# A second level of the seven-product scheme in the last stage of a transformer layer, for three of its four units

## The chip, the cores and the metric

The kernel runs on one core of one Trainium2 chip. A core has TensorE (matrix multiply; in the profile PE for the matmuls and PEld for the loads of the stationary operand), VectorE (DVE), ScalarE (ACT), GpSimd (POOL) and SyncE (SP), which here only starts transfers. The engines run their own instruction queues in order and wait for each other through semaphores. TensorE writes to PSUM, of which a partition has eight banks of 2 KB, and the other engines read it from there.

The metric is the device time in microseconds (us). Before the change the median of three runs is 739.32 us (737.54 to 741.06).

## The reference

All data is float32. `x` has 2 batches of 1024 tokens of 512 features. What is computed is one layer:

```python
xn = layernorm(x)
# attention without softmax: q, k = elu(.) + 1 of xn @ wq.T + bq and xn @ wk.T + bk, v = xn @ wv.T + bv, 16 heads of 32
KV = einsum('bhsd,bhse->bhde', k, v)
attn = (einsum('bhsd,bhde->bhse', q, KV) / (q . sum_s(k) + 1e-8)) @ wo.T + bo
# feed-forward with low-rank terms, shared and for 8 experts of rank 8, two of which are chosen for a token
gate = xn @ W_gate + lora + expert_lora
up   = xn @ W_up   + lora + expert_lora
hidden = silu(gate) * up                     # 1376 features
ffn  = hidden @ W_down + lora + expert_lora
out  = x + attn + ffn
```

The change concerns the end of it: `hidden @ W_down`, the attention's last product (queries, already divided, times a matrix that holds both KV and wo), their low-rank terms, and the sum with `x`.

## The kernel before, in words

Earlier stages normalise and transpose `x`, project keys and queries, fold KV and wo into one matrix for each batch (`kvo_dram`), and compute the hidden features. Hidden and query features are left in DRAM in a layout made for the last stage (`h_dram`, `q_dram`, and `r_dram` for the 96 hidden features that don't fill a pair of chunks).

The last stage works through four units. Unit `u = 2 b + s` is batch `b`, half `s`: 512 tokens, as two blocks of 256. The contracted features come in seven pairs of 128-row chunks: five of hidden (`NP = 5`, weights `wd[0]` to `wd[4]`) and two of queries (`NPQ = 2`, weights `kvo[0]`, `kvo[1]`). The 512 output columns are two halves of 256. So for each pair of chunks there is a product of 2 x 2 blocks by 2 x 2 blocks, and it is done with seven block products in place of eight (the scheme of Strassen in Winograd's form). A feature tile `f` holds eight blocks of 256 columns: four that are loaded, and four sums of them, which VectorE makes (`feature_sums`, L1489 to L1492). A weight tile holds eight blocks in the same manner (`block_diffs`, L1370 to L1373, on GpSimd). `H_OF` and `B_OF` tell which block each product 1 to 7 takes.

`emit_unit` keeps all seven products of a unit open in seven PSUM banks at once (`po1` to `po7`), and the eighth bank, `held3`, holds `ph`, the low-rank input (L1620). The order on TensorE is written by hand: for each of the five hidden pairs all seven products, two matmuls each (one for each 128 tokens; the moving operand is 256 weight columns wide, L1597); then `ph`; then the two query pairs; then the low-rank terms `bd_sb` x `had` and the 96 left-over features `wdr` x `hr`. VectorE, ScalarE and GpSimd then combine the seven banks into four blocks of `x` that were loaded earlier (L1641 to L1647, L1666), and SyncE stores these (L1668). In the meantime the features of the next unit arrive in a ring of nine tiles (`RING`, L1484) and get their sums. In units before the last, the sums for the next unit lie in VectorE's queue partly ahead of the read-out and partly behind it.

A float32 matmul stands in the profile as two records, each with a weight load of its own: a unit's 98 block matmuls are 196 records.

The orders of PE, DVE, ACT and POOL are those of the program text; that of SP's transfers is planned by the framework.

Of the kernel before, what the change touches and what calls it, by code (L numbers as in the profile page):

```python
# [10 lines left out]
F32 = mybir.dt.float32  # L11
# [4 lines left out]
P = 128  # L16
# [21 lines left out]
def layer_kernel(  # L38
# [41 lines left out]
    TB = 512  # L80
# [20 lines left out]
    def pool(stack, name, bufs=1, **k):  # L101
        return stack.enter_context(tc.tile_pool(name=name, bufs=bufs, reuse_waits="tile", **k))
# [78 lines left out]

    n_sa = 2 * NC + FULL + 1
    n_sat = (n_sa + SG - 1) // SG
    sat = const.tile([P, n_sat, P], F32, name="sat")
    sa = p1.tile([P, n_sat * SG, 32], F32, name="sa")


# [304 lines left out]
    class Finish:  # L492


        def __init__(self, b, pg, ksum):
            self.b, self.pg, self.ksum = b, pg, ksum
            self.made = 0
# [666 lines left out]
    def held(name, k):  # L1164
        return ps_pool[0].tile([P, TB], F32, tag=f"held{k}", name=name)
# [251 lines left out]
    def load_kvo(b):  # L1417
        ws = []
        for j in range(NPQ):
            if j == 0:  # L1420
                t = tsp.tile([P, 8, 2 * P], F32, tag="t0", name=f"kvo{b}_0")
            else:
                t = tsp.tile([P, 8, 2 * P], F32, tag="t1", name=f"kvo{b}_1")
            for half in range(2):
                nc.sync.dma_start(
                    out=t[:, 2 * half : 2 * half + 2, :].rearrange("p s n -> p (s n)"),
                    in_=kvo_dram[b][:, j + half * NPQ, :],
                )
            ws.append(t)
        return ws  # L1430


    def load_last():
        sb = tsp.tile([P, D], F32, name="sb_d")
        for k in range(SG):
            nc.sync.dma_start(out=sb[k * 32 : k * 32 + RANK, :], in_=b_down[ER:LR, :])
        wdr = tsp.tile([REST + 1, D], F32, name="wdr")
        nc.sync.dma_start(out=wdr[0:REST, :], in_=w_down[RC, :])
        nc.sync.dma_start(out=wdr[REST : REST + 1, :], in_=b_down[LR : LR + 1, :])

        bd = tsp.tile([2 * ER, D], F32, name="bd_sb")
        for i in range(2):
            nc.sync.dma_start(out=bd[i * ER : (i + 1) * ER, :], in_=b_down[0:ER, :])
        diffs = [tsp.tile([w.shape[0], HD], F32, name=n) for w, n in ((wdr, "wdr_diff"), (bd, "bd_diff"))]
        return sb, wdr, bd, *diffs
# [34 lines left out]
    def load_feature(u, i):  # L1480
        at = RING[(NF * u + i) % len(RING)]
        t = (slots if at[0] == "s" else tsp).tile([P, 8, UT], F32, tag=at, name=f"f{u}_{i}")
        b, s = divmod(u, 2)
        nc.sync.dma_start(out=t[:, 0:4, :], in_=h_dram[b][i][s] if i < NP else q_dram[b][i - NP][s])  # L1484
        feats[u, i] = t

    def feature_sums(u, i):
        t = feats[u, i]
        nc.vector.tensor_add(t[:, 4, :], t[:, 1, :], t[:, 3, :])  # L1489
        nc.vector.tensor_sub(t[:, 6, :], t[:, 0, :], t[:, 1, :])  # L1490
        nc.vector.tensor_sub(t[:, 5, :], t[:, 4, :], t[:, 0, :])
        nc.vector.tensor_sub(t[:, 7, :], t[:, 2, :], t[:, 5, :])  # L1492
# [72 lines left out]
        feature_sums(0, i)  # L1565


    p4w = pool(ctx, "p4w", bufs=2)

    H_OF = {1: 0, 2: 2, 3: 7, 4: 3, 5: 4, 6: 5, 7: 6}  # L1570
    ORDER = (1, 6, 5, 2, 7, 3, 4)
    d1, d2 = slice(0, HD), slice(HD, D)

    def load_unit(u):

        b, s = divmod(u, 2)
        hr = p4w.tile([REST + 1, 2, UT], F32, tag="hr", name=f"hr{u}")
        nc.gpsimd.memset(hr[REST : REST + 1, :, :], 1.0)
        nc.sync.dma_start(out=hr[0:REST, 0:2, :], in_=r_dram[b][s])
        xr = []  # L1580
        for g in range(2):
            t = p4w.tile([P, NQ, D], F32, tag=f"xr{g}", name=f"xr{u}_{g}")
            first = b * BT + g * TB + s * UT
            nc.sync.dma_start(out=t, in_=x[first : first + UT, :].rearrange("(q p) d -> p q d", p=P))
            xr.append((t, first))
        return hr, xr

    def emit_unit(u, loaded, last):
        hr, xr = loaded
        b, s = divmod(u, 2)  # L1590
        ps = {
            p: (bank(f"po{p}_{u}") if i < 4 else held(f"po{p}_{u}", i - 4)).rearrange("p (q n) -> p q n", n=HD)
            for i, p in enumerate(ORDER)
        }

        def term(p, q, lhsT, rhs, start=False, stop=False):
            nc.tensor.matmul(ps[p][:, q, :], lhsT, rhs, start=start, stop=stop, skip_group_check=True)  # L1597

        def products(n, w):
            f = feats[u, n]  # L1600
            for p in ORDER:
                for q in range(NQ):

                    term(p, q, f[:, H_OF[p], ts(q, P)], w[:, B_OF[p], :],
                         start=(n == 0 and q == 0), stop=(n == NF - 1 and p in (1, 6, 5)))

        for n in range(NP):
            products(n, wd[n])
            if n == 1 and not last:
                for i in range(2):  # L1610
                    load_feature(u + 1, i)
                    feature_sums(u + 1, i)

        ph = held(f"ph{u}", 3)[:, 0:UT]
        chunks = [(feats[u, j][:, 2 * half : 2 * half + 2, :], ad_sb[:, j + half * NP, 0:ER])
                  for j in range(NP) for half in range(2)]
        chunks.append((hr[0:REST], ad_sb[0:REST, FULL, 0:ER]))
        for n, (f, a) in enumerate(chunks):
            for g in range(2):
                nc.tensor.matmul(  # L1620
                    ph[g * ER : (g + 1) * ER, :], a, f[:, g, :],
                    start=(n == 0), stop=(n == len(chunks) - 1), skip_group_check=True,
                )
        had = p4w.tile([P, UT], F32, tag="had", name=f"had{u}")
        for g in range(2):
            rows = slice(g * ER, (g + 1) * ER)
            nc.vector.tensor_mul(had[rows, :], ph[rows, :], wT[b][rows, g * TB + s * UT : g * TB + (s + 1) * UT])  # L1627
        if not last:
            for i in range(2, NF):
                load_feature(u + 1, i)  # L1630
        for i in range(NPQ):
            products(NP + i, kvo[i])
        if u == 1:
            kvo[:] = load_kvo(1)

        def tmp(name):
            return p4w.tile([P, NQ, HD], F32, tag=name, name=f"{name}_{u}")

        (x1, first1), (x2, first2) = xr
        a, u2, u4 = tmp("a"), tmp("u2"), tmp("u4")  # L1640
        nc.scalar.copy(a, ps[1])  # L1641
        nc.gpsimd.tensor_add(x1[:, :, d1], x1[:, :, d1], a)  # L1642
        nc.vector.tensor_add(u2, a, ps[6])
        nc.gpsimd.tensor_add(x2[:, :, d1], x2[:, :, d1], u2)
        nc.vector.tensor_add(u4, u2, ps[5])
        nc.vector.tensor_add(x1[:, :, d2], x1[:, :, d2], u4)
        nc.vector.tensor_add(x2[:, :, d2], x2[:, :, d2], u4)  # L1647

        left = {2: (0, wdr[:, d1], bd_sb[:, d1]), 7: (1, wdr[:, d2], bd_sb[:, d2]),
                3: (0, wdr[:, d2], bd_sb[:, d2]), 4: (1, wdr_diff, bd_diff)}  # L1650

        for pp in ((2, 7), (3, 4)):
            for q in range(NQ):
                for p in pp:
                    g, _, w = left[p]
                    rows = slice(g * ER, (g + 1) * ER)
                    term(p, q, had[rows, ts(q, P)], w[rows, :])
        for p in (7, 2, 3, 4):
            g, w, _ = left[p]
            for q in range(NQ):  # L1660
                term(p, q, hr[:, g, ts(q, P)], w, stop=True)
        for t, d, p in ((x2, d2, 7), (x2, d1, 7), (x1, d1, 2), (x1, d2, 3), (x2, d1, 4)):
            first = (first1 if t is x1 else first2)

            for q in (slice(0, 1), slice(1, 2)) if last and p == 4 else (slice(0, NQ),):
                nc.vector.tensor_add(t[:, q, d], t[:, q, d], ps[p][:, q, :])  # L1666
                if p != 7 or d is d2:
                    nc.sync.dma_start(  # L1668
                        out=out[first : first + UT, d].rearrange("(q p) d -> p q d", p=P)[:, q, :], in_=t[:, q, d]
                    )  # L1670
        if u == 1:
            for t in kvo:
                block_diffs(t)
        if not last:
            for i in range(2, NF):
                feature_sums(u + 1, i)

    nxt = load_unit(0)
    for u in range(4):
        this = nxt  # L1680
        if u < 3:
            nxt = load_unit(u + 1)
        emit_unit(u, this, last=(u == 3))


# [55 lines left out]
```

## Time and profile before

| | us |
|---|---|
| median of three runs | 739.32 |
| profiled execution, its own time | 739.22 |
| its span, first to last instruction | 737.5 |
| TensorE busy | 728.4 |
| last stage, from the first `po` matmul (521.03) to the end of the span | 216.4 |
| one unit (start of the third to start of the fourth) | 52.98 |

Times inside the profile are counted from the span's start. The execution's own time lies 1.7 us above its span and 0.1 us below the median. The mean granted TensorE clock is 0.998 of the full one. In a unit of 52.98 us VectorE is busy for 17.6 us, ScalarE for 0.6 us and GpSimd for 4.2 us (in the unit that also makes the block sums of the second batch's `kvo`, 8.2 us).

### The profile page before, as it was taken

What the parts mean: (1) busy time and instruction counts of PE and PEld (TensorE: products, weight loads), DVE (VectorE), ACT (ScalarE), POOL (GpSimd) and SP (SyncE); (2) the same over time, 40 slices, a digit from 0 to 9 for tenths busy, and PEclk for the clock granted to TensorE, in tenths of its full rate; (3) what the DMA queues carried; (4) which work ended last, traced back from release to release, by engine and by line L of the source; (5) the groups of instructions that cost most, each with busy time, mean ns of one, the idle gap of its engine ahead of it and who ended that gap; (6) DMA issues with size and microseconds to landing.
All of it is one profiled execution on the core that took longest, in us unless ns stands there. A gap on an engine that the chain in (4) does not pass through costs nothing.

```text
span 737.5 us, 8743 instructions
## 1 busy us (share of the span) xinstructions
PE 728.4 (99%) x3080; PEld 490.7 (67%) x3080; DVE 485.8 (66%) x1047; ACT 195.9 (27%) x422; POOL 160.2 (22%) x206
## 2 busy tenths in 40 slices
PE   8999999999999999999999999999999999999997
PEld 6666675454433566566566666566788888878876
DVE  6788766676776688888788878878952703604303
ACT  3434413553442233333333243242100000000000
POOL 4023011202000761212212113524701003101001
PEclk9999999999999999999999999999999999999999
DMA  5243001107314001211210210352555406313001
GB/s 167 101 124 112 0 1 58 39 1 194 115 28 143 18 11 51 86 56 35 87 57 30 86 58 30 125 188 87 171 193 194 133 20 237 125 60 121 19 1 57
DMA packets 52606, 63.02 MB, mean 85 GB/s; under 512 B 9426, under 2 KB 39506, under 8 KB 52308
## 3 DMA queue, kind: packets, MB, share of 16 engines
q1 hardware_dynamic: 52034, 62.46, 26.8%
q8 instruction: 24, 0.39, 0.2%
q14 instruction: 18, 0.15, 0.1%
q10 hardware_dynamic: 530, 0.02, 0.0%
HBM read 40.71 MB, written 21.76 MB: 85 GB/s over the span
## 4 chain that ended last, share of the span: by engine, by line
PE 85%; DVE 12%; ACT 1%; issue 1%; DMA 0%; DVEq 0%
PE po L1597 26%; PE ab L1179 16%; PE b L1239 8%; PE pg L398 5%; PE pqu L772 4%; PE ph L1620 3%; PE x L1179 3%; PE b L1234 2%; PE pxa L851 2%; PE pqv L772 2%; PE pr L1073 2%; PE kua L427 2%; PE x L1234 1%; DVE r L1261 1%; DVE xn L295 1%
## 5 line engine op out<-in xcount | busy, mean ns | idle before, releaser
L1597 PE MATMUL po<-wd,f 128*128 128x256 f32 x560 | 121.8, 379 | 0.1
L1597 PEld LDWEIGHTS po<-wd,f 128*128 128x128 f32 x560 | 106.3, 190 | 14.9 <-issue 0.5
L1239 PE MATMUL b<-t,w 128*128 128x512 f32 x160 | 83.2, 601 | 0.7 <-DVE t L1261 0.7
L1627 DVE TENSOR_TENSOR had<-ph,wT 64x256 f32<-64x256 f32 x8 | 3.4, 422 | 85.4 <-PE ph L1620 85.3
L398 PE MATMUL pg<-kt,xn 128*128 128x512 f32 x128 | 58.7, 594 | 0.5 <-DVE kt L342 0.5
L1641 ACT COPY a<-po 128x512 f32<-128x512 f32 x4 | 2.3, 585 | 183.9 <-PE po L1597 183.9
L1597 PE MATMUL po<-kvo,f 128*128 128x256 f32 x224 | 49.4, 381 | 0.0
L1261 POOL TENSOR_TENSOR r<-r,r 128x512 f32<-128x512 f32 x20 | 30.1, 1524 | 84.6 <-DVE t L1261 83.0
L1597 PEld LDWEIGHTS po<-kvo,f 128*128 128x128 f32 x224 | 42.2, 190 | 7.1 <-issue 1.2
L1179 PE MATMUL ab<-ti,wi 128*128 128x256 f32 x180 | 45.4, 379 | 0.0
L1261 DVE TENSOR_TENSOR r<-r,r 128x512 f32<-128x512 f32 x60 | 44.9, 788 | 0.0
L1179 PEld LDWEIGHTS ab<-ti,w 128*128 128x128 f32 x140 | 25.2, 189 | 29.5 <-DVE r L1207 8.2
L1179 PEld LDWEIGHTS ab<-ti,wi 128*128 128x128 f32 x180 | 34.2, 190 | 13.2 <-issue 5.0
L1179 PE MATMUL ab<-ti,w 128*128 128x256 f32 x140 | 41.2, 387 | 0.5 <-DVE r L1207 0.2
L1642 POOL TENSOR_TENSOR xr<-xr,a 128x512 f32<-128x512 f32 x4 | 5.1, 1270 | 164.4 <-ACT a L1641 164.4
L398 PEld LDWEIGHTS pg<-kt,xn 128*128 128x128 f32 x128 | 23.1, 190 | 22.6 <-issue 20.6
L1212 ACT COPY r<-ab 128x256 f32<-128x256 f32 x50 | 18.6, 372 | 70.9 <-PE ab L1179 70.9
L1239 PEld LDWEIGHTS b<-t,w 128*128 128x128 f32 x160 | 29.2, 190 | 11.3 <-issue 5.9
L1207 DVE TENSOR_TENSOR r<-r,ab 128x256 f32<-128x256 f32 x50 | 20.9, 417 | 20.4 <-ACT r L1204 19.9
L1189 ACT COPY r<-ab 128x256 f32<-128x256 f32 x50 | 18.6, 373 | 48.4 <-PE ab L1179 47.1
L407 POOL TENSOR_TENSOR ksum<-ksum,kt 128x512 f32<-128x512 f32 x12 | 15.8, 1319 | 71.7 <-DVE lg L444 42.3
L1215 DVE TENSOR_TENSOR r<-r,ab 128x256 f32<-128x256 f32 x50 | 20.8, 417 | 15.7 <-ACT r L1212 15.4
(282 smaller groups left out, 1360.0 us busy)
## 6 DMA issues: line engine op xcount, KB each, us to landing
h_dram<-h SPq DMA_DIRECT2D x40, 256.0 KB
f<-h_dram SPq DMA_DIRECT2D x20, 512.0 KB
x_ring<-in_x_dram SPq DMA_DIRECT2D x16, 256.0 KB
q_dram<-qt SPq DMA_DIRECT2D x16, 256.0 KB
f<-q_dram SPq DMA_DIRECT2D x8, 512.0 KB
xr<-in_x_dram SPq DMA_DIRECT2D x8, 512.0 KB
out_dram<-xr SPq DMA_DIRECT2D x15, 256.0 KB
w<-in_w_gate_dram SPq DMA_DIRECT2D x10, 256.0 KB
```

The costliest lines, as they stand in the source:

```text
L398: nc.tensor.matmul(pg[m], xns[n][:, ts(m, P)], kt, start=(j == 0), stop=(j == TPBATCH - 1))
L772: nc.tensor.matmul(banks[c], wqs[p][:, k, ts(c, P)], tsum[b][p][:, k, :], start=(start and k == 0), stop=(k == 1), skip_group_check=True,)
L1179: nc.tensor.matmul(out, w, t, start=start, stop=True, skip_group_check=True)
L1189: nc.scalar.copy(self.r[0][:, H0], self.ua)
L1207: nc.vector.tensor_add(self.r[1][:, H1], self.r[1][:, H1], self.lo)
L1212: nc.scalar.copy(self.r[0][:, H1], self.ua)
L1215: nc.vector.tensor_add(self.r[1][:, H0], self.r[1][:, H0], self.lo)
L1234: nc.tensor.matmul(banks[m], bgu_sb[rows, cols], act[rows, :], start=starts[m], stop=True, skip_group_check=True)
L1239: nc.tensor.matmul(pb[m], ws[m][:, A_OF[p], ts(k, P)], tsum[b][p][:, k, :], start=start, stop=True, skip_group_check=True)
L1261: eng.tensor_add(to[m], t[m], v[m])
L1597: nc.tensor.matmul(ps[p][:, q, :], lhsT, rhs, start=start, stop=stop, skip_group_check=True)
L1620: nc.tensor.matmul(ph[g * ER : (g + 1) * ER, :], a, f[:, g, :], start=(n == 0), stop=(n == len(chunks) - 1), skip_group_check=True,)
```

## The change

Unit 0 keeps the old product scheme. In units 1, 2 and 3 six of the seven pairs of chunks are joined to three couples, `(0, 1)`, `(2, 3)` of hidden and the two of queries. Within each outer product a couple is again a product of 2 x 2 blocks by 2 x 2 blocks, now of 128 x 128, and is done with seven inner products. The hidden pair 4 (`SINGLE`), the left-over features and the low-rank terms stay as they are.

What follows from it in the code:

- A unit no longer keeps seven banks open. It runs product after product, in the order 1, 7, 6, 4, 5, 2, 3, each in two banks: one (`x`) for the inner products 1, 6, 5, 7 and one (`y`) for 2, 4, 3 and for all that isn't split. The outputs alternate between bank couples `A`, `B`, `C`, `E`. After each product it is read out at once (`read`): one ScalarE copy and five VectorE additions (six for product 5, which goes to two blocks of `x`).
- All features of a unit have to be resident. They stay in seven fixed tiles; the blocks of the next unit are loaded into them as soon as the old ones are used (`load_blocks`), and the outer sums are made block by block (`S12`, `S3`, `S4`).
- VectorE makes the inner sums of features (`feature_pair_sums`, in four batches for a unit) into `si`, and the inner sums of weights once, within unit 0 (`weight_sums`, into `tw` and in place). For the second batch's `kvo` this is done in steps during unit 1 and 2 (`next_kvo`).
- The low-rank terms of a unit come in two groups of four matmuls (`low_rank_pair`) in place of one of eight. `ph` follows product 1; in unit 0 it comes in two parts, so that feature tiles are free sooner.
- `x` is loaded and stored in blocks of 256 x 256 with one buffer each. `sat` and `sb_d` move to a pool that is given up before the last stage.
- GpSimd has no additions left in units 1 to 3.

```diff
+    PAIRS = ((0, 1), (2, 3), (NP, NP + 1))
+    SINGLE = NP - 1
+    EH = HD // 2
+    e0, e1 = slice(0, EH), slice(EH, HD)
...
+    tw = [p4w.tile([P, 3, 6, EH], F32, name=f"tw{k}") for k in range(len(PAIRS))]
...
+    def weight_sums(k, sl, eng=None, steps=(0, 1)):
+        eng = eng or V
+        w0, w1 = (weights(n)[:, sl, :] for n in PAIRS[k])
+        b11, b12, b21, b22 = w0[:, :, e0], w0[:, :, e1], w1[:, :, e0], w1[:, :, e1]
+        t1, t2, t4 = (t_at(k, i, sl) for i in range(3))
+        if 0 in steps:
+            eng.tensor_sub(t1, b12, b11)
+            yield
+            eng.tensor_sub(t2, b22, t1)
+            yield
+            eng.tensor_sub(t4, b21, t2)
+            yield
+        if 1 in steps:
+            eng.tensor_sub(b12, b22, b12)
...
+    BATCHES = ((1, 7), (6, 4), (5, 2), (3,))
...
+    def feature_pair_sums(u, i, ks=range(3)):
...
+        for op, m, x_, y in ((V.tensor_add, 0, 1, 3), (V.tensor_sub, 2, 0, 1), (V.tensor_sub, 1, 4, 0), (V.tensor_sub, 3, 2, 5)):
+            for k in ks:
+                at_ = (*of[k], *to[k])
+                op(to[k][m], at_[x_], at_[y])
...
+    X_AT = {1: 0, 6: 1, 5: 2, 7: 3}
+    Y_AT = {2: 0, 4: 1, 3: 2}
...
+        def products(self, p, rs):
+            for r in rs:
+                for k in range(len(PAIRS)):
+                    c = 0 if r in X_AT else 1
+                    self.term((X_AT, Y_AT)[c][r], left_of(self.u, k, r, p), right(k, r, p), c)
+
+        def main(self, p, hr=None):
+            self.products(p, (1, 2, 4))
+            f = feats[self.u, SINGLE][:, H_OF[p], :]
+            for q in range(NQ):
+                self.whole(q, f[:, ts(q, P)], weights(SINGLE)[:, B_OF[p], :])
+            if p in LEFT:
+                g, w, _ = LEFT[p]
+                for q in range(NQ):
+                    self.whole(q, hr[:, g, ts(q, P)], w)
+            self.products(p, (5, 6, 7, 3))
+
+        def read(self, *to, halves=False):
+
+            w = tmp("w", f"w{self.name}_{self.made}").rearrange("p (c n) -> p c n", n=EH)
+            self.made += 1
+            nc.scalar.copy(w[:, 0], self.x[:, 0])
+            V.tensor_add(w[:, 1], w[:, 0], self.x[:, 1])
+            V.tensor_add(w[:, 2], w[:, 1], self.x[:, 2])
+            V.tensor_add(w[:, 1::2], w[:, 1:3], self.x[:, 3:4].to_broadcast([P, 2, EH]))
...
+            if len(dst) == 1:
+                V.tensor_add(blocks[0], blocks[0], by_block(w))
+                for q in (slice(0, 1), slice(1, 2)) if halves else (slice(0, NQ),):
+                    V.tensor_add(blocks[0][:, :, q], blocks[0][:, :, q], by_block(self.y)[:, :, q])
+                    if halves:
+                        store_out(self.u, *to[0], q)
+            else:
+                V.tensor_add(w, w, self.y)
+                for v in blocks:
+                    V.tensor_add(v, v, by_block(w))
...
+    def S12(u, ns):
+        block_sum(u, 4, V.tensor_add, 1, 3, ns)
+        block_sum(u, 5, V.tensor_sub, 4, 0, ns)
+
+    def S3(u, ns):
+        block_sum(u, 6, V.tensor_sub, 0, 1, ns)
+
+    def S4(u, ns):
+        block_sum(u, 7, V.tensor_sub, 2, 5, ns)
...
+    def first_unit(hr):
...
+        products(2)
+        low_rank_sums(u, hr, (0, 1, 2))
+        for i in range(2, 5):
+            load_feature(1, i)
+        products(3)
+        both(1, (0, 1))
+        products(4)
+        low_rank_sums(u, hr, (3, 4))
+        had = low_rank_weighted(u)
+        for i in range(5, NF):
+            load_feature(1, i)
+        both(2, (0,))
+        S3(1, range(2, 4))
+        S12(1, range(2, 4))
+        feature_pair_sums(1, 0, (0, 1))
+        products(NP)
+        products(NP + 1)
...
+    def unit_of_two(u, hr, before):
+        nxt = not last_unit(u)
+        turn = next_kvo() if u == 1 else None
+        A, B, C, E_ = (
+            Out(u, n, tx, ty)
+            for n, tx, ty in (("a", "ab0", "ab1"), ("b", "x0", "x1"), ("c", "x0", "held0"), ("e", "held1", "held2"))
+        )
+
+        A.main(1)
+        before()
+        if turn:
+            turn[0](slice(0, 2))
+        S12(u, range(NF) if u > 1 else range(5, NF))
+        low_rank_sums(u, hr, tuple(range(NP)))
+        A.read((0, 0))
+        had = low_rank_weighted(u)
+        if nxt:
+            hr_next = load_rest(u + 1)
+            load_blocks(u + 1, slice(0, 2))
+        feature_pair_sums(u, 1)
+
+        B.main(7, hr)
+        low_rank_pair(had, (3, E_), (7, B))
+        if turn:
+            turn[1]()
+        B.read((1, 1))
+
+        A.main(6)
+        S4(u, range(NF))
+        feature_pair_sums(u, 2, (0,))
+        A.read((1, 0))
+        feature_pair_sums(u, 2, (1, 2))
+
+        B.main(4, hr)
+        low_rank_pair(had, (2, C), (4, B))
+        if nxt:
+            load_blocks(u + 1, slice(3, 4))
...
+        B.read((1, 0))
+        store_out(u, 1, 0)
...
+        A.main(5)
+        feature_pair_sums(u, 3)
+        if nxt:
+            S3(u + 1, range(NF))
+        A.read((0, 1), (1, 1))
...
+        if turn:
+            turn[2]()
+
+        C.main(2, hr)
+        if nxt:
+            load_blocks(u + 1, slice(2, 3))
+            feature_pair_sums(u + 1, 0)
+        C.read((0, 0))
...
+        E_.main(3, hr)
...
+        def after():
+            E_.read((0, 1), halves=not nxt)
+            if nxt:
+                store_out(u, 0, 1)
+                load_out(u + 1, 0, 1)
+            if turn:
+                turn[3]()
```

`after` of one unit is the next one's `before`, so the last product of a unit is read out behind the first product of the next. `both(k, ...)` in unit 0 makes the weight sums of couple `k`. `turn[1]` to `turn[3]` are the steps of `next_kvo`: two additions of 256 columns; four of 256 and nine narrow ones; two of 256 and nine narrow ones.

## The prediction

> **What bounds the kernel now.** I read the page's busy line first, then the last stage in order of time, then the pace of single records.
>
> ```profile
> PE 728.4 (99%) x3080; PEld 490.7 (67%) x3080; DVE 485.8 (66%) x1047; ACT 195.9 (27%) x422; POOL 160.2 (22%) x206
> ...
> PE   8999999999999999999999999999999999999997
> PEld 6666675454433566566566666566788888878876
> DVE  6788766676776688888788878878952703604303
> ```
>
> PE is full in every slice, the last eleven (the last stage) too, while DVE falls to a third. The timeline of PE alone, from the third unit on:
>
> ```profile
> 627.37 30.38 PE L1597 MATMUL po<-wd,f 128*128 128x256 f32 x140
> 657.68 4.54 PE L1620 MATMUL ph<-f,ad_sb 128*64 128x256 f32 x40
> 662.05 0.60 PE L1620 MATMUL ph<-hr,ad_sb 96*64 96x256 f32 x4
> 662.59 12.35 PE L1597 MATMUL po<-kvo,f 128*128 128x256 f32 x56
> 674.87 1.34 PE L1597 MATMUL po<-bd_sb,had 64*128 64x256 f32 x9
> ...
> 676.80 2.86 PE L1597 MATMUL po<-wdr,hr 97*128 97x256 f32 x12
> 679.49 1.03 PE L1597 MATMUL po<-wdr_diff,hr 97*128 97x256 f32 x4
> 680.35 30.38 PE L1597 MATMUL po<-wd,f 128*128 128x256 f32 x140
> ```
>
> Each row begins where the one before ends, so start to start is the cost. A unit is 680.35 - 627.37 = 52.98 us: hidden pairs 30.31, `ph` 4.91, query pairs 12.28, low-rank 1.93, left-over features 3.55. A record of 256 columns costs 30.31 / 140 = 0.2165 us. No wait separates the rows; the last stage is worth what PE's work is worth.
>
> **The matmuls.** A couple within one outer product was 4 matmuls of 256 columns, 8 records. It becomes 7 matmuls of 128 columns, 14 records. If cost went by columns that would be 7/8. But each record brings its own load of 128 x 128 weights, and the change has twice as many loads for each column. So the price hangs on the pace of records of 128 columns with new weights each. The kernel has such a stretch, the 16 matmuls of `pv` (L540), timeline of PE, then of PEld:
>
> ```profile
> 99.19 3.73 PE L540 MATMUL pv<-gt,wv_sb 128*128 128x128 f32 x32
> 102.76 0.60 PE L305 MATMUL pt<-ident,xn 128*128 128x128 f32 x4
> ```
>
> ```profile
> 98.97 3.20 PEld L540 LDWEIGHTS pv<-gt,wv_sb 128*128 128x128 f32 x27
> ```
>
> 32 records in 102.76 - 99.19 = 3.57 us: 0.1116 us each. A single load of these lasts 0.192 us, longer than the pace; 27 of them (the window cuts the rest off) fit in 3.20 us, so loads overlap each other and don't set a pace of 0.19.
>
> Here a rule of the Trainium skill speaks against the change: "TensorE: Matmul & The Clock Gate", section "Back-to-back issue gap", says that in a stream of load and matmul pairs the spacing at 128 columns is about 81 ns, where the matmul alone would take about 56, because the load counts too. Scaled as an estimate to float32 (half of 0.2165, times 81/56) that would be 0.157 us a record, 294 records 46.0 us, and a unit about 10 us longer than before. The row says 0.1116, for this type and shape, on this chip; I take the row.
>
> A unit then has 3 couples x 7 products x 7 matmuls = 147 matmuls, 294 records: 294 x 0.1116 = 32.8 us. The single pair keeps 28 records: 6.1 us. Together 38.9, where 30.31 + 12.28 = 42.6 stood: 3.7 us less.
>
> **Added on TensorE.** Where the used part of the array changes, a little is lost: the 16 low-rank records run side by side in pairs, 8 x 0.2165 = 1.73, and take 1.93, so 0.2 us a change. The low-rank group is now two (0.2 more) and the left-over features sit inside the products (up to 0.2): 0.4 us a unit. In unit 0 `ph` is in two parts, 0.3 us. Many matmuls have a wait. Those that are already fulfilled cost nothing measurable: the query pairs take 12.28 us in the third unit, where several wait for two semaphores, and 727.85 - 715.57 = 12.28 in the fourth, which has none of these. At 128 columns there is less slack to start a load early, so 20 starts of a product at 0 to 0.2 us: 0 to 4 us, taken as 0, the row's value.
>
> So a unit is 52.98 - 3.7 + 0.4 = 49.7 us; three units save 3 x 3.3 = 10.0, unit 0 costs 0.3.
>
> **VectorE.** This is the cover of all the sums. Its price, from the timeline of DVE in unit 0:
>
> ```profile
> 533.55 0.68 DVE L1249 TENSOR_TENSOR h<-h,r 128x512 f32<-128x512 f32 x1
> 534.15 0.68 DVE L1249 TENSOR_TENSOR h<-h,t 128x512 f32<-128x512 f32 x1
> ...
> 545.13 0.42 DVE L1489 TENSOR_TENSOR f<-f 128x256 f32<-128x256 f32 x1
> 545.47 0.41 DVE L1490 TENSOR_TENSOR f<-f 128x256 f32<-128x256 f32 x1
> 545.80 0.41 DVE L1491 TENSOR_TENSOR f<-f 128x256 f32<-128x256 f32 x1
> 546.25 0.43 DVE L1492 TENSOR_TENSOR f<-f 128x256 f32<-128x256 f32 x1
> ```
>
> Start to start: 512 columns 0.60, 256 columns 0.335, and 0.12 more when the operation needs the one just before it (545.80 to 546.25). From these two, 128 columns 0.20, 384 0.47 and 768 0.87 (estimates). A unit: 28 outer sums x 0.335 = 9.4; inner sums 36 x 0.335 + 12 x 0.20 = 14.5; six read-outs of 0.3 + 0.3 + 0.455 + 0.72 + 0.72 = 2.5 and one of 3.1: 18.1; `had` 0.9 (its row). Sum 42.9 us in 49.7 of PE, against 17.6 before. GpSimd falls silent, so the 0.94 us that such a sum took beside GpSimd's work (timeline, 524 to 533) doesn't return.
>
> Less than PE in sum is not enough: both queues are in order. PE from a unit's start: product 1 to 5.6, `ph` to 10.5, 7 with its low-rank to 18.0, 6 to 23.5, 4 to 31.0, 5 to 36.6, 2 to 43.0, 3 to 49.7. Tightest is unit 1 into unit 2, where the sums of the second `kvo` come on top. DVE ends the read-out of 5 at 40.3 (its product ends at 36.6), `turn[2]` (4 x 0.335, three of 0.47, six of 0.20, some dependent: 4.3) at 44.6, the first inner sums of unit 2 at 48.6, read-outs of 2 and 3 at 53.6, `turn[3]` (2.8) at 56.4, `S12` (14 x 0.335 = 4.7) at 61.1, the read-out of unit 2's product 1 at 63.6, `had` at 64.5, the next batch of inner sums at 68.5. Who waits: product 1 of unit 2 needs its inner sums at 49.7 + 2.9 (there at 48.6); the low-rank group behind product 7 needs `had` at 66.6 (there at 64.5: 2.1 us of cover); product 6 needs the read-out of product 1 at 67.7 and inner sums from 70.6. Every need is met; the least cover is about 2 us on a queue busy for some 28. Unit 2 into 3 lacks the 7 us of `turn` steps.
>
> In unit 0 DVE is done with what it had before at about 545.5. Then come weight sums, a couple being 4 x (0.20 + 0.87) and some dependence, 4.6: 550.1 and 554.7 for the first two; `had` behind `ph` 557.4; the first three quarters of the query couple (3.3) 560.7; 6 outer sums of features 562.8; 8 inner 565.6. There the read-out starts, where it started at 564.8 before, with PE at work until 574.4. What follows is as long as before but for 4 inner sums and 1.1 of weights; unit 1's product 1 needs the latter from 572.7 on, as I count it. So nothing added here is on the path; if this queue were 3 us later it would begin to be.
>
> **Transfers.** SP's queue now has its waits inside the unit. `S3` needs blocks 0 and 1 at 34.8; their seven loads wait for `ph` (10.5) and take some 0.5 us each to issue. Block 3 is loaded behind product 4 (31) and needed by `S12` at 56; block 2 behind product 2 (39 to 43) and needed by `ph` at 55.3. Behind these stand the loads of `kvo`, which wait for product 3 (49.5), and behind them the stores of blocks read out earlier and the loads of `x` for the next unit: the block for the read-out of product 1 is issued at about 54.3 and wanted at 61.8. The seven loads of one block step are 0.9 MB, some 5 us at the 190 GB/s that several of the last slices moved, so all have room. I add nothing for this.
>
> **The end.** Before, the last PE record ends at 732.47 + 1.03 = 733.5, the last addition at 734.3, the span at 737.5: the store. Now product 3's read-out is last: its `x` bank is complete three matmuls (0.67 us) before PE ends, then 0.455, 0.72, 0.455 and 0.335 follow: the last addition is 1.5 us behind PE in place of 0.8, if only the last inner product is waited for; 2.4 if ScalarE's copy (0.37) and the two first additions wait for the whole bank. I take 1.0 us more.
>
> **Sum.** -10.0 + 0.3 + 1.0 = -8.7 us on the span of 737.5, so 728.8; the same on the median of 739.3 gives 730.6.
>
> **The rivals.**
> (a) Loads of weights become the bound: slower. For it: twice the loads for each column, the rule above, and 32 records are the longest such stretch that the trace shows, where the change runs 300. Against: the row. The change breaks even on the whole where a record costs 0.1116 + 8.7 / 882 = 0.1215 us, only 9% more. At 0.135 the loss is 882 x 0.0234 - 8.7 = 12 us: 751.
> (b) VectorE comes late and PE waits for it. For it: 43 us and more of 49.7, a chain of 28 us without a pause and 2 us of cover, additions that read PSUM and wait for a copy. Against: the count above. If each operation is 15% dearer, the seam is 4 us late in unit 2 and perhaps 1 us in others: 735.
> (c) Product starts cost 0.2 us each, the upper end above, with the longer end (0.9 more): gain 3.8, 735.5, no difference that can be told.
> (d) Records run at 0.1083, half of those with 256 columns, and the end is hardly longer: 882 x 0.0033 = 2.9 less, and 0.7: 727.0.
>
> **How the numbers follow.** The likeliest (count as made, within 1.5 us) 0.56, (d) 0.12, (b) 0.13, (c) 0.09, (a) 0.10. A measurement of this kernel tells about 0.5% from no change, 3.7 us: 735.6 to 743.0. Faster: the likeliest, (d), most of (b) and half of (c): 0.83. Same: 0.09. Slower: 0.08. Range: from (d), 726.0, to the upper side of (b) and (c), 736.5; what is left out is (a) and a little at both ends. The likeliest alone: 729 to 732.5.
>
> **What would show it.** Right: rows of PE with 128 x 128 records at about 0.112 us start to start; units 1 to 3 at 49.7 us; no wait of PE for DVE over a few tenths; DVE 80 to 90% busy in the last stage; last addition 1.5 to 2.4 us behind the last matmul. Wrong: PEld busy all the time and PE's records further apart (a); waits of PE for `had`, `si` or a bank not yet read (b); a gap at each start of a product (c).

## The result, and the profile after

| | before | after |
|---|---|---|
| median of four runs, us | 740.12 (737.54 to 741.06) | 731.06 (730.01 to 733.87) |
| profiled execution, us | 739.22 | 732.03 |
| its span, us | 737.5 | 730.2 |
| last stage, first `po` matmul to the end of the span, us | 216.4 | 208.9 |
| one unit of the changed ones, us | 52.98 | 49.95 |
| last matmul record's end to the end of the span, us | 4.0 | 5.2 |

The ratio of the times is 0.9889, with a 95% interval of 0.9848 to 0.993. The forecast was 730.6 and "faster by over 0.5%" at 0.83. In a second comparison, on one chip with some of the experiments below, the same kernel had 731.75 (six runs) where the kernel before had 740.77 (eleven runs): 0.9895 (0.9871 to 0.992).

The busy line and the rows of slices of PE, PEld and DVE on the page of after, with the same columns as before:

```profile
PE 719.9 (99%) x3458; PEld 494.6 (68%) x3458; DVE 580.0 (79%) x1326; ACT 199.8 (27%) x440; POOL 147.3 (20%) x192
...
PE   8999999999999999999999999999999999999997
PEld 6666676454433556666666666666688899899896
DVE  6788766776777688878878878968888889998874
```

TensorE is still full everywhere. VectorE, which fell to a third in the last stage, is now busy for 84 to 92% of units 0 to 2 and for 72% of the last. By unit, with the columns window, length, busy time of PE, PEld, DVE, ACT and POOL (instructions behind each), granted TensorE clock, DMA share and GB/s:

```profile
521.00:575.03 54.03, 53.88 (x276) 44.67 (x275) 48.23 (x96) 2.12 (x4) 14.69 (x16) 1.00 0.43 140
575.03:624.98 49.95, 49.95 (x399) 45.86 (x398) 42.13 (x117) 1.86 (x7) 1.04 (x2) 1.00 0.52 161
624.98:674.93 49.95, 49.95 (x400) 45.86 (x399) 45.79 (x131) 1.86 (x7) 0.00 (x0) 1.00 0.40 122
674.93:724.90 49.97, 49.97 (x400) 45.84 (x398) 36.05 (x97) 1.85 (x7) 0.00 (x0) 1.00 0.12 38
```

Units 1 and 2 take 49.95 us each, and so does unit 3, whose window ends about where one more record would start. VectorE has 42.1, 45.8 and 36.1 us of work in them, but PE is busy for the whole of each window, so nothing that VectorE does shows in its pace. The rows of PE at the start of unit 1 are these:

```profile
575.70 0.61 PE L1747 MATMUL pya<-wd,f 128*128 128x128 f32 x4
576.14 0.39 PE L1747 MATMUL pya<-kvo,f 128*128 128x128 f32 x2
576.37 0.61 PE L1747 MATMUL pya<-wd,f 128*128 128x128 f32 x4
576.81 0.39 PE L1747 MATMUL pya<-kvo,f 128*128 128x128 f32 x2
577.03 1.03 PE L1747 MATMUL pya<-wd,f 128*128 128x256 f32 x4
```

Six records, one inner product over the three couples, take 576.37 - 575.70 = 0.67 us: 0.1115 us each. The end of the kernel, all engines in order of time; the bracket tells the idle time before an instruction and what ended it:

```profile
724.46 0.27 ACT L1774 COPY we<-pxe 128x128 f32<-128x128 f32 x1 [6.15 <-PE pxe L1747]
724.67 0.39 PE L1747 MATMUL pye<-kvo,si_3b 128*128 128x128 f32 x2
724.76 0.29 DVE L1775 TENSOR_TENSOR we<-we,pxe 128x128 f32<-128x128 f32 x1 [3.84 <-ACT we L1774]
...
726.66 0.75 DVE L1787 TENSOR_TENSOR xr<-xr,pye 128x256 f32<-128x256 f32 x2
```

The copy starts only when the whole `x` bank is complete. PE ends at 724.67 + 0.39 = 725.06, the last addition at 727.41, 2.35 us behind it.

The median fell by 9.06 us and the stage by 7.5. The kernels are the same up to the stage; where the rest comes from is told under what had not been expected. The stage is the cleaner measure, and the experiments are read by it and by the length of a unit.

### The profile page after: what moved, and what is told of

Its sections match the earlier page's. It is cut to its first block, busy times and chain, and to the rows that moved or that the text cites. A ratio compares the mean times of both kernels' runs of the same rounds, so it can differ in the third digit from the quotient of the medians.

```text
span 730.2 us, 9892 instructions
## 1 busy us (share of the span) xinstructions
PE 719.9 (99%) x3458; PEld 494.6 (68%) x3458; DVE 580.0 (79%) x1326; ACT 199.8 (27%) x440; POOL 147.3 (20%) x192
## 4 chain that ended last, share of the span: by engine, by line
PE 84%; DVE 12%; ACT 1%; issue 1%; DMA 0%; DVEq 0%; ACTq 0%
PE ab L1179 16%; PE b L1239 8%; PE po L1875 7%; PE pg L398 5%; PE pqu L772 4%; PE pya L1747 4%; PE pxa L1747 3%; PE pyb L1747 3%; PE ph L1615 3%; PE x L1179 3%; PE pxb L1747 2%; PE pyc L1747 2%; PE b L1234 2%; PE pqv L772 2%; PE pxa L851 2%; PE pr L1073 2%
## 5 line engine op out<-in xcount | busy, mean ns | idle before, releaser
L1212 ACT COPY r<-ab 128x256 f32<-128x256 f32 x50 | 18.6, 373 | 71.5 <-PE ab L1179 71.5
L1215 DVE TENSOR_TENSOR r<-r,ab 128x256 f32<-128x256 f32 x50 | 20.9, 418 | 16.2 <-ACT r L1212 15.8
L1189 ACT COPY r<-ab 128x256 f32<-128x256 f32 x50 | 18.6, 373 | 48.5 <-PE ab L1179 47.0
L1875 PE MATMUL po<-wd,f 128*128 128x256 f32 x140 | 30.9, 380 | 0.1
L407 POOL TENSOR_TENSOR ksum<-ksum,kt 128x512 f32<-128x512 f32 x12 | 15.8, 1320 | 71.7 <-DVE lg L444 42.3
L1200 ACT COPY r<-ab 128x256 f32<-128x256 f32 x50 | 18.6, 373 | 40.8 <-PE ab L1179 40.8
L1818 DVE TENSOR_TENSOR f<-f 128x256 f32<-128x256 f32 x84 | 29.4, 423 | 0.1
L1875 PEld LDWEIGHTS po<-wd,f 128*128 128x128 f32 x140 | 26.4, 190 | 4.4 <-issue 0.5
L1179 PE MATMUL ab<-xnT,w 128*128 128x256 f32 x100 | 29.4, 390 | 0.0
L1179 PE MATMUL ab<-xnT,wi 128*128 128x256 f32 x100 | 28.1, 379 | 0.0
L1179 PEld LDWEIGHTS ab<-xnT,w 128*128 128x128 f32 x100 | 18.1, 189 | 10.8 <-issue 4.3
```

The lines of the kernel that those rows point to most:

```text
L1179: nc.tensor.matmul(out, w, t, start=start, stop=True, skip_group_check=True)
L1189: nc.scalar.copy(self.r[0][:, H0], self.ua)
L1215: nc.vector.tensor_add(self.r[1][:, H0], self.r[1][:, H0], self.lo)
L1818: op(t[:, at, :], t[:, x_, :], t[:, y, :])
```

## The experiments

The theory: TensorE alone sets the time of the units; a record of 128 columns with new weights costs 0.1115 us, so a couple saves 56 x 0.2165 - 98 x 0.1115 = 1.2 us a unit; VectorE, the transfers and the waits are covered. The main rivals: (a), that loads of weights hold the records back, (b), that VectorE does, and that some of the gain was lost again at places that can be named. All kernels but those under "The order of the last product" ran once, so they are read by the length of a unit inside the profile and not by their times.

### Twice the loads without the new scheme

The kernel before, with each of the unit's matmuls at L1597 of 256 columns issued as two of 128 with the same weights. The arithmetic is unchanged. The edit also splits the low-rank terms and the left-over features.

```diff
         def term(p, q, lhsT, rhs, start=False, stop=False):
-            nc.tensor.matmul(ps[p][:, q, :], lhsT, rhs, start=start, stop=stop, skip_group_check=True)
+            for k in range(2):
+                c = ts(k, P)
+                nc.tensor.matmul(ps[p][:, q, c], lhsT, rhs[:, c], start=start and k == 0, stop=stop, skip_group_check=True)
```

> The kernel before, with each matmul of 256 columns on the seven pairs of chunks issued as two of 128 columns with the same stationary block: the same columns, twice the weight loads, nothing else changed. My theory (a record of 128 columns costs 0.1116 us): a unit is 392 x 0.1116 - 42.6 = 1.1 us longer, 54.1 us, and the whole some 4.6 us longer. Loads as the bound at 0.157 us a record: a unit of about 72 us. Columns alone (half of 0.2165): a unit of 52.8 us.

Measured: 744.83 us, span 743.0; the kernel before beside it 738.18. The rows of PE from unit 1 to unit 2:

```profile
574.83 31.43 PE L1599 MATMUL po<-wd,f 128*128 128x128 f32 x280
606.19 4.54 PE L1622 MATMUL ph<-f,ad_sb 128*64 128x256 f32 x40
...
629.56 31.43 PE L1599 MATMUL po<-wd,f 128*128 128x128 f32 x280
```

280 records in 606.19 - 574.83 = 31.36 us: 0.1120 each, against 0.1083 for half a record of 256 columns. The unit takes 54.73 in place of 52.98, +1.75: 1.05 in the hidden pairs, 0.42 in the query pairs, 0.28 in the terms that the edit split as well; without these it is 54.45 against the 54.1 that was expected for the pairs. So twice the loads cost 3.4%, where rival (a) needed 12% (0.1215) to break even. At the 0.157 estimated above from the Trainium skill's rule, the unit would have taken some 72 us. So loads do not cost what rival (a) needs, in the kernel before or in the one after; what they do cost is told under "What sets 0.1115".

### Two couples in place of three

Only the hidden couples go through the inner scheme; the query couple is done as it was, and VectorE leaves out the sums that belong to it. The result is the same sum.

```diff
         def products(self, p, rs):
             for r in rs:
-                for k in range(len(PAIRS)):
+                for k in range(2):
...
-            f = feats[self.u, SINGLE][:, H_OF[p], :]
-            for q in range(NQ):
-                self.whole(q, f[:, ts(q, P)], weights(SINGLE)[:, B_OF[p], :])
+            for n in (SINGLE, NP, NP + 1):
+                f = feats[self.u, n][:, H_OF[p], :]
+                for q in range(NQ):
+                    self.whole(q, f[:, ts(q, P)], weights(n)[:, B_OF[p], :])
```

> The changed kernel with the second level for the two couples of hidden alone; the couple of queries is done with 8 records of 256 columns for each outer product. My theory (each couple saves 8 x 0.2165 - 14 x 0.1113 = 0.174 us a product): a unit is 7 x 0.174 = 1.2 us longer than 49.95, 51.2 us. Theory that the gain comes from elsewhere (resident features, the product order, GpSimd's silence): a unit stays at 50.

Measured: 735.63, span 733.8; unit 677.17 - 626.07 = 51.10, 1.15 more than with three. The count gives 1.2. Continued in a straight line, three couples are worth 3.45 a unit; the units gained 3.03. By that line some 0.42 is lost whatever the number of couples. This is an extrapolation from two points, not a measurement.

### VectorE without the inner sums

The inner sums of features are left out (the matmuls take raw blocks in their place), so that this part of the output is not the layer's. TensorE issues the same records.

```diff
     def feature_pair_sums(u, i, ks=range(3)):
-
+        return
...
         if r in (3, 5, 6, 7):
+            return (f0, f1)[r % 2][:, 0:P]
```

> The changed kernel without the inner sums of features: VectorE does not make them, and the inner products 3, 5, 6 and 7 read raw blocks in their place, so the result is not the layer's. TensorE has the same instructions. My theory (the sums lie under TensorE's work): units 1 to 3 stay at 49.95 us within 0.1, while VectorE's busy time falls by about 14 us a unit. Theory of a late VectorE: the units become shorter by what TensorE waited.

Measured: 733.67, span 731.9, stage 731.9 - 522.98 = 208.9, as after. Its unit 2, in the columns of the windows above:

```profile
626.65:676.61 49.96, 49.96 (x401) 45.87 (x400) 30.77 (x82) 1.86 (x7) 0.00 (x0) 1.00 0.38 123
```

VectorE has 15 us less to do there (30.77 in place of 45.79) and the unit takes 49.96 in place of 49.95. VectorE costs nothing as it is.

### VectorE made late

The size of the cover was the weakest number of the forecast: 2.1 us at the point where the low-rank terms of unit 2 need `had`. So VectorE is held up just ahead of `had`, in that unit alone, by additions of 512 columns that go nowhere, two and eight of them (the run with eight came first):

```diff
         A.read((0, 0))
+        if u == 2:
+            z = tmp("r", "late")
+            V.memset(z, 0.0)
+            for _ in range(2):
+                V.tensor_add(z, z, z)
         had = low_rank_weighted(u)
```

> The changed kernel with a memset and two dependent additions of 512 columns ahead of had in unit 2: about 0.3 + 2 x 0.72 = 1.7 us more on VectorE. By the run with eight additions, where TensorE waited about 3 us of 6.1, the cover is some 3 us: unit 2 stays at 49.95 us. If the cover were not there (the wait of that run came from something else), unit 2 becomes longer.

> The changed kernel with a memset and eight dependent additions of 512 columns on VectorE's scratch ahead of had in unit 2, about 0.3 + 8 x 0.72 = 6.1 us of extra work at the place of least cover. In the changed kernel's trace had is there at 639.0 and the low-rank group that needs it starts at about 642.1: a cover of 3.1 us. My theory: unit 2 becomes 6.1 - 3.1 = 3.0 us longer (53.0 us), units 1 and 3 stay. Theory of much cover: nothing changes. Theory of none: 6.1 us longer.

With two: span 730.0, unit 2 is 674.70 - 624.75 = 49.95, and PE waits for nothing there. With eight: 735.15, span 733.4, unit 2 is 678.09 - 624.87 = 53.22, +3.27. The waits of that kernel, of PE and of PEld (what waits for what: us in total, times, the longest):

```profile
PE pye L1747 <- DVE had L1627: 2.7, 1, 2.7
```

```profile
PEld pye L1747 <- DVE had L1627: 2.9, 1, 2.9
```

Of PE there is no other wait in the stage. VectorE comes to `had` 6.35 us later in the unit than in the kernel after, and the unit is longer by what goes beyond the cover. In the kernel after, `had` is ready at 639.0 and the low-rank group starts at about 642.1, so the cover is 3.1 us. Rival (b) was a real danger, 3 us away, and not what happened.

### What sets 0.1115

The count was right; was its reason? A record of 128 columns might cost what its columns cost (0.108 and a little), or its load might be a floor under it. Three kernels with less work in two of the three couples tell this. All leave a part of the products out, so only their times mean anything.

First, only 64 of the 128 moving columns in two couples of three, with weights as before:

```diff
...
             o = v[:, out, :] if isinstance(out, int) else v.rearrange("p (e q) n -> p q e n", q=NQ)[:, out[0]]
+            if narrow:
+                o, rhs = o[:, 0:64], rhs[:, 0:64]
...
-                    self.term((X_AT, Y_AT)[c][r], left_of(self.u, k, r, p), right(k, r, p), c)
+                    self.term((X_AT, Y_AT)[c][r], left_of(self.u, k, r, p), right(k, r, p), c, narrow=k > 0)
```

> The changed kernel with two of the three couples computing only the first 64 of 128 columns in their inner products; the rest of their sum is left out, so the result is not the layer's. 196 of a unit's 294 inner records move 64 columns, each with a full load of 128 x 128 weights. If columns set the pace of 128-column records, these cost about 0.056 us and a unit falls by 196 x 0.056 = 11 us to 39 us (or to what VectorE allows, some 43 to 46). If the load of weights is a floor just below 0.11, which is what I think, they cost 0.105 to 0.11 and a unit stays above 48.5 us.

Measured: 733.33, span 731.5; unit 676.42 - 626.63 = 49.79, only 0.16 less, though 196 of its records move half the columns. Its rows of PE (a row joins the records of the first and the second couple, and shows the shape of the first):

```profile
677.10 0.61 PE L1749 MATMUL pya<-wd,f 128*128 128x128 f32 x4
677.54 0.39 PE L1749 MATMUL pya<-kvo,f 128*128 128x64 f32 x2
677.76 0.61 PE L1749 MATMUL pya<-wd,f 128*128 128x128 f32 x4
```

677.76 - 677.10 = 0.66 us for six records, as before. So the moving columns do not set the pace at 128 and below. Next, the same with 64 columns of the stationary operand too (and, to keep VectorE out of it, without the inner sums):

```diff
+            if narrow:
+                o, lhsT, rhs = o[0:64, 0:64], lhsT[:, 0:64], rhs[:, 0:64]
```

> The changed kernel without the inner sums of features (raw blocks in their place, so that VectorE can't be the bound), and with two of the three couples in a smaller form: 64 of the 128 columns of weights and 64 of the 128 tokens as the stationary block. The rest is left out, so the result is not the layer's. As in the run with narrow moving operands, 196 of 294 records are small, but here each loads 64 columns of stationary data in place of 128. If the load of 128 stationary columns is what holds a record at 0.111 us, small records cost about 0.056 to 0.07 us and a unit falls to 39 to 42 us. If it is a price for each record whatever its size, a unit stays at about 49.8 us. I expect the first.

This one missed. It was to take 39 to 42 us a unit, and took 55.3 (642.14 - 586.88, between the last rows of `ph` in units 1 and 2); 748.98 in all, slower than the kernel before, with less work. Its rows:

```profile
577.09 0.75 PE L1750 MATMUL pya<-wd,f 128*128 128x128 f32 x4
577.67 0.28 PE L1750 MATMUL pya<-kvo,f 128*64 128x64 f32 x2
577.88 0.75 PE L1750 MATMUL pya<-wd,f 128*128 128x128 f32 x4
```

Six records, two wide and four small, take 577.88 - 577.09 = 0.79 in place of 0.67, and nothing is waited for. Within each six the shape changes twice. If that is what costs, grouping the records by shape must bring the time back. So the same work once more, with the couples as the outer loop:

```diff
-            for r in rs:
-                for k in range(len(PAIRS)):
+            for k in range(len(PAIRS)):
+                for r in rs:
```

> As the run with small stationary blocks (64 of 128 weight columns, 64 of 128 tokens for two couples, no inner sums, so the result is not the layer's), but the couples are the outer loop: records of one shape stand together, 6 or 8 large and then 12 or 16 small, in place of 2 and 4. A unit has the same records. In that run a change of shape was mixed with the price of a small record. If a change of shape is what cost there and the 128 columns of the load are the floor at 0.111, a unit falls well below 49.95 us, towards 42. If a record has a floor whatever it loads, a unit stays at or above 49.8 us.

Measured: 714.76, span 713.0; unit (663.71 - 576.85) / 2 = 43.4. Its rows of PE, where wide records give way to small ones:

```profile
593.45 0.39 PE L1750 MATMUL pya<-tw,f 128*128 128x128 f32 x2
593.76 0.33 PE L1750 MATMUL pxa<-wd,f 128*64 128x64 f32 x2
593.93 0.28 PE L1750 MATMUL pya<-wd,f 128*64 128x64 f32 x2
594.05 0.28 PE L1750 MATMUL pya<-tw,f 128*64 128x64 f32 x2
594.16 0.28 PE L1750 MATMUL pxa<-kvo,f 128*64 128x64 f32 x2
594.28 0.28 PE L1750 MATMUL pya<-kvo,f 128*64 128x64 f32 x2
594.40 0.28 PE L1750 MATMUL pya<-tw,f 128*64 128x64 f32 x2
```

From 594.05 to 594.40 six small records take 0.35 us, 0.058 each; at the change, the two wide ones take 0.31 where two cost 0.22, and the first two small ones 0.17 where two cost 0.12. Without any price for changes, this unit would take 49.95 - 196 x (0.1115 - 0.058) = 39.5. Grouped, with 28 changes of shape (four in each of seven products), it takes 43.4: (43.4 - 39.5) / 28 = 0.14 us a change. Alternating, with 98 (fourteen in each), it takes 55.3: 15.8 / 98 = 0.16 a change. One price of about 0.15 fits both.

So with 64 moving columns a record costs 0.111 us behind a load of 128 stationary columns and 0.058 behind one of 64. The floor goes with the width of the load, not with the columns that move, and a change of that width costs some 0.15 us (in the run with 64 moving columns alone, mixed shapes cost nothing). In this sense rival (a) was right: the loads do set the pace in the kernel after. But their floor lies at 0.111, only 3% above half of 0.2165.

### The order of the last product

The end took 1.2 us more than before, since product 3's `x` bank is complete only just before PE ends. In the last product of the last unit the inner products that go to the `x` bank are put first; nothing is left out.

```diff
         def main(self, p, hr=None):
-            self.products(p, (1, 2, 4))
+            end = self.u == 3 and p == 3
+            self.products(p, (1, 5, 6, 7, 2, 4, 3) if end else (1, 2, 4))
...
-            self.products(p, (5, 6, 7, 3))
+            if not end:
+                self.products(p, (5, 6, 7, 3))
```

> The changed kernel, but the last product of the last unit runs its inner products 1, 5, 6, 7 first and 2, 4, 3, the single pair and the left-over features behind them, so that the x bank is complete about 3.7 us before TensorE ends and the read-out's first four steps lie under TensorE. The last addition should come 0.8 us behind the last matmul in place of 2.35, and the span from the first po matmul to the end be 1.5 us shorter than the changed kernel's 208.9: 207.4. A rival: the copy waits for something later than its bank, and nothing changes.

> The changed kernel as it is, on the same chip as the run with the reordered end: from the first po matmul to the end 208.9 us, units 1 to 3 at 49.95 us, a ratio to the kernel before of about 0.989.

Measured: 731.09 (728.82 to 732.07, six runs) beside 731.75 (730.34 to 733.54) for the kernel after; ratios to before 0.9877 (0.9855 to 0.99) and 0.9895 (0.9871 to 0.992). The medians can't be told apart. The profiled executions can: stage 728.3 - 520.97 = 207.3 against 729.8 - 520.94 = 208.9. The end of the reordered kernel:

```profile
721.05 0.27 ACT L1776 COPY we<-pxe 128x128 f32<-128x128 f32 x1 [3.08 <-PE pxe L1747]
...
723.69 1.03 PE L1747 MATMUL pye<-wdr,hr 97*128 97x256 f32 x4
724.75 0.75 DVE L1789 TENSOR_TENSOR xr<-xr,pye 128x256 f32<-128x256 f32 x2 [1.61 <-PE pye L1747]
```

The copy starts 3.7 us ahead of PE's end in place of 0.6, and the last addition ends at 725.50, 0.8 us behind PE, as in the kernel before. From PE's end to the span's end it is 3.6 us in place of 5.2. This version is the best of those that compute the whole layer, by 1.6 us of the stage.

## Why the prediction was right

By its own steps, in us:

| step | predicted | measured |
|---|---|---|
| a record of 128 columns | 0.1116 | 0.1115 |
| a unit | 49.7 | 49.95 |
| three units | -10.0 | -9.1 |
| unit 0 | +0.3 | +0.36 |
| the end | +1.0 | +1.2 |
| the stage | -8.7 | -7.5 |
| the profiled span | 728.8 | 730.2 |

**The pace of the record** was the number on which the sign hung, and the stretch of `pv` gave it to 0.1%. The rule in the Trainium skill's "TensorE: Matmul & The Clock Gate", section "Back-to-back issue gap", had spoken for 0.157, as an estimate scaled to float32; neither the kernel after nor the split one bears that out. But why the price is 0.1115 the forecast did not know: it took a row and gave no reason for it. It is the load's floor, with half of 0.2165, 0.108, just under it. The same page's section "LDWEIGHTS" makes a load's time proportional to its columns and not to the rows; for 128 columns an estimate by it is 107 ns and for 64 it is 53. The floor measured here is 111 ns for 128 columns, and records with 64 took 58 ns. (A load's own record lasts 0.19 us, as the row of `pv` shows, but loads overlap, and what counts is the pace of the stream.) With that rule beside it, the step would have rested on more than one row.

**The price of the unit** is the term that was mis-sized: of the 3.7 us saved in the pairs, 0.7 was lost again, not 0.4. The rows of unit 1 show where. In us, as forecast and as measured: the pairs 38.9 and 39.47 (what the rest leaves of 49.95), `ph` 4.91 and 4.90, the two low-rank groups 2.13 and 2.13, the left-over features up to 3.75 and 3.45. So the left-over features inside the products cost nothing more, and the pairs cost 0.6 more than the count. These are the rows around the first low-rank group, of PE and of PEld:

```profile
591.87 0.39 PE L1747 MATMUL pyb<-kvo,si 128*128 128x128 f32 x2
592.19 0.48 PE L1747 MATMUL pye<-bd_sb,had 64*128 64x256 f32 x1
...
593.25 0.71 PE L1747 MATMUL pxa<-wd,f 128*128 128x128 f32 x4
593.80 0.39 PE L1747 MATMUL pxa<-kvo,f 128*128 128x128 f32 x2
594.02 0.61 PE L1747 MATMUL pya<-wd,f 128*128 128x128 f32 x4
```

```profile
593.25 0.52 PEld L1747 LDWEIGHTS pxa<-wd,f 128*128 128x128 f32 x4 [0.33 <-issue]
593.69 0.30 PEld L1747 LDWEIGHTS pxa<-kvo,f 128*128 128x128 f32 x2
```

Ahead of the group two records take 592.19 - 591.87 = 0.32 us where two cost 0.22, and behind it six take 594.02 - 593.25 = 0.77 where six cost 0.67. The same 0.1 is lost on both sides of `ph` and of the second group: six times in a unit, 0.6 us in all. The forecast knew that a change of the used part of the array costs something, but it read the price from the low-rank rows alone. PEld shows what is different there: in the stream a load starts 0.11 us ahead of its matmul (593.69 and 593.80), and behind the change it starts together with it (593.25). Why it is not started earlier, no run here shows.

Rival (c) is not this: a start of a product costs nothing as such. Product 4 of unit 1 follows product 6 directly, and its first six records take 599.58 - 598.91 = 0.67 us.

**VectorE.** Counted from start to start 42.9 us in a unit, measured busy 42.1, 45.8 and 36.1 in the three. The instruction with the least cover was named right, and its time nearly so: `had` in unit 2 (in the run with eight additions it is the only thing that PE waits for) was to be done at 64.5 us after the start of unit 1, so at 639.5. In the kernel after, the timeline of DVE has:

```profile
638.14 0.87 DVE L1627 TENSOR_TENSOR had<-ph,wT 64x256 f32<-64x256 f32 x2
```

It ends at 639.0, and the cover is 3.1 instead of 2.1 us. In unit 0 the read-out was foreseen from 565.6 and began at 566.3. PE waited for VectorE nowhere in the last stage.

**The end.** The forecast left open whether the copy waits for the last inner product alone or for the whole bank (1.5 or 2.4 us behind PE) and took a number between. The dearer one happened: 2.35, which is 1.6 more than the 0.8 of the kernel before. From PE's end to the span's end it is only 1.2 more, since from the last addition to the end it took 2.8 us in place of 3.2; why, no run shows. That the guess of 1.0 came so near is partly luck.

**The transfers** were costed at nothing. PE is busy throughout units 1 to 3, so no transfer held it up. VectorE did wait for one in unit 1, 0.97 us for a block of `x` at 582.50, within its cover. How much later a transfer could come was not tried.

**What the median hid.** The span came out 1.4 us above the forecast and the median only 0.5 above. The stage misses by 1.2; the agreement of the medians is partly the luck of how runs start, as told below.

Of the rivals, (d) is out (0.1115, not 0.1083), (b) is refuted by runs, (a) is right in that loads set the pace and wrong in what it costs, and (c) is out: the 0.6 us a unit lie at the changes of shape.

## What to carry to other kernels

A second level of a seven-product scheme pays where the matmuls shrink and the weight loads are still covered: halving the columns from 256 to 128 cost 3% for each column, halving them again would gain nothing, since the record then stands at its load's 0.111 us. Look in the trace for a stretch of the very shape that a change makes more of, and check what holds that stretch: columns, loads or changes of shape. Where a product is read out at once, put what is read first at the front of the last product.

## What had not been expected of the hardware

**A change of the stationary operand's width costs about 0.15 us,** more than a record. Less work in a mixed order took 748.98 us, and in a grouped one 714.76. Of widths, only 128 against 64 columns was tried. The rows of the kernel after show a like price for fewer rows: a low-rank group, with 64 rows in place of 128, costs 0.2 us in its own rows and 0.2 in those beside it, for two changes. The left-over features, with 97 rows, show none. In the grouped run, too, the first load behind a change starts together with its matmul (593.76 for both) and the next ones 0.06 us ahead of theirs:

```profile
593.76 0.19 PEld L1750 LDWEIGHTS pxa<-wd,f 128*64 128x64 f32 x2
593.87 0.20 PEld L1750 LDWEIGHTS pya<-wd,f 128*64 128x64 f32 x2
```

**The start of the kernel decides a spread of 3.4 us between the profiled runs.** The same code runs there in all kernels. In order of time, the twelve records of 256 columns at L359 and what follows them, in the kernel before, in the split one and in the one with 64 moving columns:

```profile
8.00 4.51 PE L359 MATMUL pk<-wk_sb,xnT 128*128 128x256 f32 x12
12.34 0.60 PE L305 MATMUL pt<-ident,xn 128*128 128x128 f32 x4
```

```profile
8.04 2.90 PE L359 MATMUL pk<-wk_sb,xnT 128*128 128x256 f32 x12
10.77 0.61 PE L305 MATMUL pt<-ident,xn 128*128 128x128 f32 x4
```

```profile
9.54 5.07 PE L359 MATMUL pk<-wk_sb,xnT 128*128 128x256 f32 x12
14.44 0.60 PE L305 MATMUL pt<-ident,xn 128*128 128x128 f32 x4
```

They take 4.34, 2.73 and 4.90 us, that is 0.36, 0.23 and 0.41 a record, where the full pace is 0.2165. The stage starts at 521.03, 519.76 and 523.18 in turn: the differences stay, to 0.3 us, for the next 500 us. From 8 to 12 us the mean granted clock is 0.59 in the kernel before and 0.57 in the one after, and 1.00 in the split one, which is what the first two paces ask for. In the third the trace's record of the clock begins only at 14.0 us, at the full clock; up to there the clock isn't recorded. Its pace asks for half of it until then: 4.4 us at half and 0.5 at full make the twelve records. So there the clock is argued and not shown. The Trainium skill's "TensorE: Matmul & The Clock Gate", section "Part 1: The HAM clock gate (the "warmup" mystery)", says that the moment at which the clock is raised varies from run to run with the phase of a free-running window; a difference of this kind fits it. For a change in a late stage, compare stages and not spans.
